# Attention kernel on one core: the read of turned probabilities moved behind three more key pages in each turn, apart from the read of the next queries

## Chip, core and metric

The kernel runs on one core of one Trainium2 chip. The metric is the device time of one execution in microseconds (us). Three runs before the change gave 1230.02, 1235.01 and 1238.47 us; the median, 1235.01 us, is the number to move.

## What is computed

Eight sequences of 128 rows and 512 columns pass through two layers. The first applies one of eight adapter matrices per sequence and a small mixture of low-rank experts. The second, where nearly all the time goes, is attention over a paged cache, followed by a gated low-rank layer. Cut to the attention, the reference is:

```python
q, k, v = x @ Wq.T, x @ Wk.T, x @ Wv.T           # 32 query heads, 8 key and value heads, 128 wide
q, k = rope(rmsnorm(q, q_norm_w)), rope(rmsnorm(k, k_norm_w))
kc = k_cache[block_table].reshape(B, 512, 8, 128) # 16 pages of 32 keys for each sequence
vc = v_cache[block_table].reshape(B, 512, 8, 128)
scores = einsum("bqhd,bkhd->bhqk", q, repeat(concat(kc, k), 4)) * SCALE
probs = softmax(where(valid, scores, -1e30))
o = einsum("bhqk,bkhd->bqhd", probs, repeat(concat(vc, v), 4))
out = o.reshape(B, S, 4096) @ Wo.T
```

All arithmetic is 32-bit.

## The kernel before, in words

The attention is cut into 64 units, one for each sequence and key head. Two units in a row share a sequence and form a step `st`; a step's keys are one tile `kt` of 16 pages (buffer count 2) and one tile `vt` of values. A key head serves four query heads, h = 0 to 3. The function `iteration(u)` (line 1225) is one turn of a software pipeline over the units: in turn u the scores and the softmax of unit u are made, the projections for a unit about three ahead, the product with the values for unit u - 2 at the end of the turn, and the output product of unit u - 3. Nothing is reordered by a scheduler: each engine runs its instructions in the order in which the Python code issues them. The lines that matter are these.

- **Scores.** `scores` on TensorE: lines 837 (against the cached keys `kt`) and 840 (against the new keys), into two PSUM buffers. VectorE takes them out with the mask and the row minimum (850), ScalarE exponentiates (861), VectorE inverts the sum (866), GpSimd scales (867), and VectorE turns the probabilities in 32 by 32 blocks into `pb` (872).
- **The way through DRAM.** The block transpose turns inside blocks only; the order of the blocks is mended by a round trip through a DRAM tile `px`. `exchange_out(u)` (877) writes `pb` there at the end of turn u as four transfers of 400 KB (886), two issued by SyncE (SP) and two by ScalarE (ACT). In turn u + 1, `exchange_in(u)` (892) reads it back, both reads from SP: the turned queries and key of unit u + 2 as `qkb` (896, 320 KB) and the turned probabilities of unit u as `pT` (899, 1280 KB, two buffers, by the parity of u). `qkb` is put into place by ScalarE at the end of the turn (`heads_qk`, 906) and is needed by the first scores of the next turn. `pT` is needed by the product with the values (919) at the end of the next turn, some 14 us after it has landed.
- **One buffer `pb`.** There is one `pb`, so in turn u the first thing that VectorE writes into it, the turned queries of unit u + 2 (`blocks_qk`, 823, called at h = 2), waits until all four writes of turn u - 1 have landed. Behind it on VectorE stand the turned probabilities (872), the adds that take the projections out of PSUM (264, which free the bank that TensorE's next projection, 261, writes) and the scores of h = 3 (850).
- **Pages.** `gather` (185) issues the key pages of the step after this one from SP, 32 KB each (196), every one behind a read of its page number into a register. An even turn issues ten pages, an odd turn six: the first three ahead of `exchange_in`, the rest behind it. The last six pages of a step are issued in the odd turn, and TensorE reads that `kt` in the first score product of the even turn that follows.
- **Other traffic from SP.** In one odd turn out of two a partial output is read back (146), in the other it is written (1142). GpSimd issues the value gathers (206) and the weights.
- **Completion semaphores.** In the built program, the transfers of SP and ACT take eight completion semaphores in rotation, in the order in which the code issues them. A transfer whose semaphore was last used by another one waits, ahead of its issue and in its engine's queue, until that other one has landed. Which transfer stands eight places ahead of which therefore depends on the order of the code.

The main loop ends with turn 66; turns 60 and later have no pages or fewer, and the second layer's last part is mixed into them.

Of the kernel before, what the change touches and what calls it, by code (L numbers as in the profile page):

```python
# [9 lines left out]
F32 = mybir.dt.float32  # L10
# [6 lines left out]
P = 128  # L17
# [16 lines left out]
QD = P // 32  # L34
HN = DM // 2
PW = REP * (LC + 1) * 32
# [22 lines left out]
def adaln_ffn_kernel(  # L59
# [25 lines left out]
    nc = tc.nc  # L85
# [33 lines left out]
        out=nw, in_=norm_w.rearrange("o (t d) -> o t d", t=2).to_broadcast([P, 2, D])  # L119
# [65 lines left out]
    def gather(step, first=0, end=NPP):  # L185
        hf, b = divmod(step, B)
        if first == 0:
            kv_t[step] = (
                kvp.tile([P, NPP, GH, PSIZE], F32, tag="kt", name=f"kt_{step}"),
                kvp.tile([P, LC, GH * D], F32, tag="vt", name=f"vt_{step}", bufs=3),  # L190
            )
        kt, vt = kv_t[step]
        for j in range(first, end):
            at = b * NPP + j
            page = nc.sync.value_load(pg[0:1, at : at + 1])
            nc.sync.dma_start(
                out=kt[:, j, :, :].rearrange("p g t -> p (g t)"),
                in_=kc[hf, ds(page, 1)].rearrange("o p f -> p (o f)"),
            )
# [198 lines left out]
    with ExitStack() as l0:  # L398
# [70 lines left out]
        for i in range(QD):  # L469
            nc.gpsimd.dma_start(  # L470
                out=vpg[i * 32 : (i + 1) * 32], in_=vpages[i : i + 1].to_broadcast([32, B * LC])
# [319 lines left out]
    with ExitStack() as l1:  # L791
        wk1 = l1.enter_context(tc.tile_pool(name="l1_1", bufs=1))
# [7 lines left out]
        p_t, pb_t, pT_t, den_t, o_t, oT_t, y_t = {}, {}, {}, {}, {}, {}, {}  # L800
        mask_t, px_t, qkb_t, qk_out = {}, {}, {}, {}
# [89 lines left out]

        def exchange_in(u):
            m = px_t.pop(u).rearrange("k b i f -> (k b) i f")
            if u + 2 in range(3, NU):
                qkb = wk1.tile([P, QD, NH * 32], F32, tag="qkb", name=f"qkb_{u + 2}")
                nc.sync.dma_start(out=qkb, in_=m[:, :, PW:])
                qkb_t[u + 2] = qkb
            pT = wk1.tile([P, QD, PW], F32, tag=f"pT{u % 2}", name=f"pT_{u}")
            nc.sync.dma_start(out=pT, in_=m[:, :, :PW])
            pT_t[u] = pT  # L900

        def heads_qk(u):

# [278 lines left out]
        def room(b):  # L1182
            at = [0]

            def sb(n, shape):
                if n in ("yT", "zg", "zT"):
                    v = room_t[n, b if n != "yT" else b % 2]
                    return v if len(shape) == 2 else v.rearrange("p (c s) -> p c s", c=shape[1])
                at[0] += -(-shape[1] // 8) * 8
                return room_t["small", b % 2][:, at[0] - -(-shape[1] // 8) * 8 :][:, : shape[1]]  # L1190

            def psum(n, shape):
                t = bank("kv" if n == "z" else "q", f"f{n}_{b}")
                if len(shape) == 2:
                    return t[:, : shape[1]]
                t = t[:, : shape[1] * shape[2]]
                return t.rearrange("p (c s) -> p c s", c=shape[1])

            return sb, psum
# [25 lines left out]
        def iteration(u):  # L1225

            on = lambda v: 0 <= v < NU
            fb = LAST.get(u)
            r, group = u % 16, (u // 16 + 1) * GH
            f = room(fb) if fb is not None else None  # L1230

            if u % 4 == 3:
                k, j, four = (u + 5) // 4, 0, True
            elif u % 4 == 0:
                k, j, four = (u + 4) // 4, 0, False
            elif u % 4 == 1:
                k, j, four = (u + 3) // 4, 1, True
            else:
                k, j, four = (u + 2) // 4, 1, False
# [3 lines left out]
            st = u // GH  # L1243
            pages = on(u) and 1 < st + 1 < NQ * B
            first, end = ((0, 10), (10, NPP))[u % GH]
            if pages:
                gather(st + 1, first, first + 3)
            if on(u - 1):
                exchange_in(u - 1)
            if pages:  # L1250
                gather(st + 1, first + 3, end)
            if pages:
                gather_v(st + 1, u % GH * LC // GH, (u % GH + 1) * LC // GH)
            if on(u + 3) and u % GH == 1:
# [100 lines left out]
        for u in range(NU + 3):  # L1355
            iteration(u)
# [160 lines left out]
```

## Time and profile before

| what | us |
|---|---|
| median of three runs | 1235.01 |
| profiled execution, its own time | 1233.53 |
| span of that execution | 1231.8 |
| key pages, 32 KB each, issued one by one | 512 |
| a pair of turns in the loop | 31 to 36 |
| SP waits at the writes to `px` for an earlier write to `px` | 60.5 in 24 waits |
| bytes moved | 302.71 MB, 246 GB/s over the span |

How to read it: times in a timeline are counted from the span's start, and the execution's own time is 1.7 us more than its span. The granted TensorE clock was 0.999 of full speed, so no part of the time is a slower clock. Busy shares of TensorE contain a modelled end, so where its stalls matter the distance between starts of its instructions is used. The waits of SP's queue (marked SPq) cost nothing by themselves; they matter by when a transfer starts.

### The profile page before, as it was taken

Reading aid. Unit: us, or ns where it says so; the run is one execution under the profiler, and the core shown is the slowest. Engines: PE = TensorE matmul, PEld = TensorE weight load, DVE = VectorE, ACT = ScalarE, POOL = GpSimd, SP = SyncE. Lnnn points to the kernel's source line nnn. Section 1 sums busy time; section 2 is a strip of 40 time slices with the busy share of each in tenths; the row PEclk is TensorE's granted clock in tenths of the full one; section 3 lists DMA queues with packets and bytes.
Section 4 is the critical chain, followed back from the end, with each engine's and each line's share of the span. In section 5 each row is a group of like instructions: output and inputs, shape, how many; then the busy total and the mean of one; then the engine's idle time right before and its main releaser. Section 6 shows DMA issues by size and latency. Waiting matters only on the chain.

```text
span 1231.8 us, 16787 instructions
## 1 busy us (share of the span) xinstructions
PE 1205.3 (98%) x4159; PEld 708.9 (58%) x4159; DVE 908.4 (74%) x2099; ACT 504.0 (41%) x1457; POOL 718.5 (58%) x800
## 2 busy tenths in 40 slices
PE   8999989999999999999999999999999999999998
PEld 7765545565555555555555565555555555655544
DVE  2545778878888787788887787888786888876622
ACT  1344444444444443444444344444443444443211
POOL 2443678778755576577646675687556775742100
PEclk9999999999999999999999999999999999999999
DMA  8822688888888988898889888988888888878742
GB/s 305 298 88 95 215 243 247 257 258 277 253 251 257 288 253 234 282 281 282 248 260 284 267 241 277 291 285 253 255 262 262 263 263 257 263 259 235 218 130 95
DMA packets 206837, 302.71 MB, mean 246 GB/s; under 512 B 84820, under 2 KB 120405, under 8 KB 205845
## 3 DMA queue, kind: packets, MB, share of 16 engines
q1 hardware_dynamic: 174964, 208.72, 53.8%
q10 hardware_dynamic: 18720, 52.32, 16.2%
q0 software_dynamic: 13056, 40.60, 9.7%
q8 instruction: 33, 0.54, 0.2%
q14 instruction: 64, 0.52, 0.1%
HBM read 185.64 MB, written 115.93 MB: 245 GB/s over the span
## 4 chain that ended last, share of the span: by engine, by line
PE 50%; DMA 19%; POOL 8%; DVE 8%; issue 6%; SPq 4%; ACT 4%; ACTq 0%; DVEq 0%; POOLq 0%
DMA px<-pb 14%; PE o L919 10%; PE p L261 9%; PE s L837 9%; PE y L1044 6%; DVE pb L872 3%; DMA kt<-in_kc 3%; POOL p L867 3%; PE bp L548 2%; PE op L1404 2%; PE s L840 2%; PE cp L526 2%; ACT sq L310 2%; PE y L1057 2%; PE fz L733 2%
## 5 line engine op out<-in xcount | busy, mean ns | idle before, releaser
L861 ACT ACTIVATE p<-p,low 128x640 f32<-128x640 f32 x256 | 211.7, 827 | 467.2 <-DVE den L866 299.2
L867 POOL TENSOR_SCALAR p<-p,den 128x640 f32<-128x640 f32 x256 | 209.6, 819 | 275.0 <-DVE den L866 273.6
L261 PE MATMUL p<-wqkv,xo 128*128 128x384 f32 x784 | 283.1, 488 | 4.7 <-DVE c L264 4.6
L850 DVE CUSTOM_DVE_ANT_0 p<-s,mask,rs 128x640 f32<-128x640 f32 x256 | 222.0, 877 | 81.7 <-PE s L840 80.6
L837 PE MATMUL s<-kt,qkT 128*128 128x512 f32 x504 | 259.4, 596 | 11.3 <-DVE low L850 4.9
L919 PE MATMUL o<-pT,vt 128*128 128x512 f32 x512 | 231.6, 595 | 0.0
L872 DVE STREAM_TRANSPOSE pb<-p 128x640 f32<-128x640 f32 x256 | 211.0, 824 | 18.8 <-POOL p L867 18.8
L1044 PE MATMUL y<-wo,oT 128*128 128x256 f32 x784 | 206.6, 380 | 0.5 <-DVE yp L1113 0.5
L261 PEld LDWEIGHTS p<-wqkv,xo 128*128 128x128 f32 x784 | 147.6, 190 | 76.2 <-DVE c L264 11.3
L840 PEld LDWEIGHTS s<-qkT 128*128 128x128 f32 x504 | 95.8, 190 | 120.5 <-issue 120.5
L919 PEld LDWEIGHTS o<-pT,vt 128*128 128x128 f32 x512 | 98.0, 191 | 111.3 <-issue 96.3
L206 POOL DMA_INDIRECT vt<-in_vc,vrow x128 | 141.9, 1108 | 34.4 <-issue 32.0
L837 PEld LDWEIGHTS s<-kt,qkT 128*128 128x128 f32 x504 | 93.1, 190 | 85.8 <-issue 38.3
L1044 PEld LDWEIGHTS y<-wo,oT 128*128 128x128 f32 x784 | 131.8, 191 | 9.4 <-PE s L840 0.6
L310 ACT ACTIVATE sq<-c 128x128 f32<-128x128 f32 x320 | 98.8, 309 | 8.1
L840 PE MATMUL s<-qkT 128*128 128x128 f32 x504 | 96.8, 274 | 0.0
L823 DVE STREAM_TRANSPOSE pb<-ca 128x640 f32<-128x640 f32 x60 | 50.4, 840 | 55.7 <-DMA px<-pb 53.4
L316 POOL TENSOR_TENSOR rs<-ss,mhalf 128x5 f32<-128x5 f32 x64 | 83.7, 1308 | 5.3
L942 ACT COPY oT<-o 128x512 f32<-128x512 f32 x64 | 37.5, 585 | 91.0 <-PE o L919 65.4
L314 POOL TENSOR_SCALAR ss<-ss,eps 128x5 f32<-128x5 f32 x64 | 20.7, 323 | 77.6 <-ACT sq L310 77.4
L919 PE MATMUL o<-pT,vn 128*128 128x512 f32 x128 | 65.4, 592 | 0.0
L264 DVE TENSOR_TENSOR c<-c,p 128x384 f32<-128x384 f32 x84 | 44.9, 534 | 21.3 <-PE p L261 21.0
(193 smaller groups left out, 1409.1 us busy)
## 6 DMA issues: line engine op xcount, KB each, us to landing
pT<-px SPq DMA_DIRECT2D x64, 1280.0 KB
px<-pb ACTq DMA_DIRECT2D x120, 400.0 KB
px<-pb SPq DMA_DIRECT2D x120, 400.0 KB
qkb<-px SPq DMA_DIRECT2D x61, 320.0 KB
kt<-in_kc SPq DMA_DIRECT2D x512, 32.0 KB
wqkv<-in_wqkv POOLq DMA_DIRECT2D x32, 384.0 KB
wo<-in_wo POOLq DMA_DIRECT2D x17, 512.0 KB
yd<-yp SPq DMA_DIRECT2D x12, 512.0 KB
```

The costliest lines, as they stand in the source:

```text
L206: nc.gpsimd.indirect_dma_start(out=kv_t[step][1][:, c, :], out_offset=None, in_=vc, in_offset=bass.IndirectOffsetOnAxis(ap=vrow[:, hf, at ...
L261: nc.tensor.matmul(out=ps, lhsT=xo[:, pr, x, c, :], rhs=w[:, c, :], start=(c == 0), stop=(c == 1))
L310: nc.scalar.activation(sq, cs[:, at : at + D], AF.Square, accum_out=ss[:, h : h + 1])
L316: nc.gpsimd.tensor_tensor(rs, ss, mhalf, ALU.pow)
L837: nc.tensor.matmul(out=s[:, :L], lhsT=qkT[:, h, :], rhs=kt[:, :, g % GH, :], start=True, stop=True)
L840: nc.tensor.matmul(out=s[:, L:NK], lhsT=qkT[:, h, :], rhs=qkT[:, REP, :], start=True, stop=True)
L850: nc.vector.tensor_tensor_reduce(out=p, in0=s_t.pop((u, h))[:, :NK], in1=mask_t[st], scale=rs_t[u][:, h : h + 1], scalar=BIG, op0=ALU.add, ...
L861: nc.scalar.activation(p, p, AF.Exp, bias=low, scale=-1.0, accum_out=den)
L867: nc.gpsimd.tensor_scalar(p_t[u, h], p_t[u, h], den, 1.0, ALU.mult, ALU.mult)
L872: nc.vector.transpose(pb_t[u][:, :, h * w : (h + 1) * w].rearrange("p i (j a) -> p j i a", a=32), p_t.pop((u, h)).rearrange("p (j i a) -> ...
L919: nc.tensor.matmul(out=o, lhsT=vt[:, c, j * D : (j + 1) * D] if c < LC else vn_t.pop(u), rhs=pT[:, c], start=(c == 0), stop=(c == LC),)
L1044: nc.tensor.matmul(out=y_t["y"][:, half * HN : (half + 1) * HN], lhsT=part(key)[:, i * S : (i + 1) * S], rhs=wo_t[:, slot(w, key[0] // (B ...
```

## The change

The two reads of `exchange_in` become two functions. `exchange_qk(u - 1)` reads `qkb` where both reads stood before, behind the turn's first three pages. Three more pages follow, then `exchange_in(u - 1)` with the read of `pT` alone, then the pages that are left: four in an even turn, none in an odd one. No transfer is added, removed or resized.

```diff
         def exchange_in(u):
             m = px_t.pop(u).rearrange("k b i f -> (k b) i f")
+            pT = wk1.tile([P, QD, PW], F32, tag=f"pT{u % 2}", name=f"pT_{u}")
+            nc.sync.dma_start(out=pT, in_=m[:, :, :PW])
+            pT_t[u] = pT
+
+        def exchange_qk(u):
+            m = px_t[u].rearrange("k b i f -> (k b) i f")
             if u + 2 in range(3, NU):
                 qkb = wk1.tile([P, QD, NH * 32], F32, tag="qkb", name=f"qkb_{u + 2}")
                 nc.sync.dma_start(out=qkb, in_=m[:, :, PW:])
                 qkb_t[u + 2] = qkb
-            pT = wk1.tile([P, QD, PW], F32, tag=f"pT{u % 2}", name=f"pT_{u}")
-            nc.sync.dma_start(out=pT, in_=m[:, :, :PW])
-            pT_t[u] = pT
...
             if on(u - 1):
+                exchange_qk(u - 1)
+            if pages:
+                gather(st + 1, first + 3, first + 6)
+            if on(u - 1):
                 exchange_in(u - 1)
             if pages:
-                gather(st + 1, first + 3, end)
+                gather(st + 1, first + 6, end)
```

In the rotation of the semaphores the three pages now stand between `qkb` and `pT`. In the built program before, in 29 even turns (2 to 58) one of SP's two writes to `px`, mostly the first, comes eight places behind ACT's first write of the same turn and waits for it to land, and in most of these turns ACT's second write waits for the turn's `pT`. In the program after, the writes to `px` of the even turns to 58 stand behind pages, but for SP's second write, which stands behind the turn's `pT`.

## Prediction

> **What bounds the kernel now.** I read the busy row of the page first, then the loop's window, then what TensorE waited for.
>
> ```profile
> PE 1205.3 (98%) x4159; PEld 708.9 (58%) x4159; DVE 908.4 (74%) x2099; ACT 504.0 (41%) x1457; POOL 718.5 (58%) x800
> ```
>
> ```profile
> core 0: us, PE busy (x) PEld busy (x) DVE busy (x) ACT busy (x) POOL busy (x), PEclk, DMA share, GB/s
> ...
> 166.00:1120.00 954.00, 943.44 (x3129) 553.06 (x3127) 769.99 (x1688) 420.65 (x1248) 631.72 (x677) 1.00 0.86 263
> ```
>
> TensorE is the bound: in the loop it is busy 943.4 of 954 us at full clock. So a gain can only come out of its gaps, while a loss has no ceiling. Busy time hides part of a gap (the modelled end runs into it), so I also summed the distances between starts of matmuls above the median distance of their kind: 16.8 us from 200 us to the end, 8.2 us from 150 to 200 us. A little over 20 us is the ceiling; I ask which of it the change can reach.
>
> TensorE's own waits, and a place where one happens (the turn boundary into turn 50):
>
> ```profile
> PE s L837 <- DMA kt<-in_kc: 4.4, 4, 1.9
> ```
>
> ```profile
> 924.04 1.02 PE L919 MATMUL o<-pT,vn 128*128 128x512 f32 x2
> 926.94 1.10 PE L837 MATMUL s<-kt,qkT 128*128 128x512 f32 x2 [1.88 <-DMA kt<-in_kc]
> ```
>
> The first score product of an even turn waits for key pages. SP's queue in the odd turn before it:
>
> ```profile
> 916.98 0.54 SPq L896 DMA_DIRECT2D qkb<-px  x1
> 917.57 0.62 SPq L899 DMA_DIRECT2D pT<-px  x1
> 918.72 2.94 SPq L196 DMA_DIRECT2D kt<-in_kc  x3
> 923.68 0.81 SPq L886 DMA_DIRECT2D px<-pb  x2
> ```
>
> The last three pages are issued right behind the 1280 KB of pT, on the same queue. In the packet records pT's last packet ends at 925.6 and the last page's at 925.9, 5.5 us after its issue; the product starts 1.0 us later.
>
> **Part 1: pages ahead of pT.** For every even turn I took the start of its first score product less the start of the last value product before it. With nothing to wait for this is 0.43 us (turns 32, 38, 40 and others). In 18 of the 29 even turns from 4 to 60 it is more, up to 2.47 (turn 50); the excess adds up to 8.7 us. In each of these 18 the last page lands 0.8 to 1.25 us ahead of the product, and the queries lie ready (qkT's copy ends 3 us or more earlier), so it is the pages. After the change the last page of an odd turn goes out at qkb + 0.54 + 0.52 (register read) + 2 x 0.85 = 2.8 us, for turn 49 at 919.7. Pages with no large transfer ahead of them land in about 1.3 to 2.5 us: 922.2 at the latest, where TensorE asks at 924.9. In turn 21, the tightest I found, 461.1 against 463.4. The margin is over 2 us, so all of it goes: **-8.7 us** (ends -8.7 and, if another wait stands right behind, 0). In even turns three pages of ten go ahead as well, but these are asked for a turn later and gain nothing.
>
> **Part 2: the writes of even turns.** SP's queue in turn 30:
>
> ```profile
> 605.50 0.54 SPq L896 DMA_DIRECT2D qkb<-px  x1
> 606.09 0.62 SPq L899 DMA_DIRECT2D pT<-px  x1
> 607.24 6.00 SPq L196 DMA_DIRECT2D kt<-in_kc  x7
> 615.83 0.92 SPq L886 DMA_DIRECT2D px<-pb  x2
> ```
>
> ACT's two writes go out at 612.38 and 612.73, so the data were ready; SP is through with its pages at 613.24 and yet issues at 615.83. By the wait list of the built program its first write shares a completion semaphore with ACT's first write and waits for that to land. The bandwidth while only ACT's writes move (turn 30), and while both queues' do (turn 29):
>
> ```profile
> core 0: us, PE busy (x) PEld busy (x) DVE busy (x) ACT busy (x) POOL busy (x), PEclk, DMA share, GB/s
> 597.30:602.00 4.70, 4.31 (x18) 3.05 (x19) 4.67 (x11) 1.07 (x2) 4.07 (x4) 1.00 0.98 308
> ...
> 613.30:617.40 4.10, 4.10 (x18) 2.72 (x17) 3.57 (x9) 0.93 (x2) 3.58 (x4) 1.00 0.99 199
> ```
>
> The DMA share is full in both, but the rate is 199 GB/s for one queue and 308 for two. The Trainium skill (DMA: Bandwidth & Descriptors, "Issuing engines are not separate DMA queues") speaks against a gain here: transfers of all engines share the same 16 DMA engines, so a second issuer saves issue time only. By that rule the 1.6 MB land as late as before, part 2 is 0 and the sum below 1228.3; by the rows two queues move them half again as fast. I take the rows. After the change this wait is gone: SP's first write goes out at 613.4, its second when pT has landed (issued at 608.65, and 5.2 us later, since its 6.1 us now hold 0.9 us behind qkb: 613.9). 1.1 us of ACT alone moves 0.22 MB, the other 1.38 MB at 308 take 4.5 us: landing near 618.9 instead of 621.65.
>
> Who waits for that: VectorE at line 823 of the next, odd turn, in every odd turn, 1.7 us on average.
>
> ```profile
> DVE pb L823 <- DMA px<-pb: 53.4, 33, 3.2
> ```
>
> The worst, in turn 35, and what it does to TensorE through the add of line 264:
>
> ```profile
> 689.54 0.84 DVE L823 STREAM_TRANSPOSE pb<-ca 128x640 f32<-128x640 f32 x1 [3.20 <-DMA px<-pb]
> ```
>
> ```profile
> 691.60 1.56 PE L261 MATMUL p<-wqkv,xo 128*128 128x384 f32 x4 [0.88 <-DVE c L264]
> ```
>
> VectorE itself is not the bound; only TensorE's stalls behind it count. By distance of starts they are 2.56 (turn 3), 0.70 (13), 0.60 (19), 1.05 (35) and 0.56 (51), 5.5 us in all. Not all goes: **-4 us** (ends -5.5 and 0).
>
> **Part 3: what comes later.** pT is now issued three pages later: 3 x 0.85 us, about 2.6. It has the time: turn 30's pT lands at 612.2 and is read at 626.65. SP issues as many instructions as before, so what stands behind pT (pages, line 146, line 1142, the writes) gets its turn no later. But pT's data move later, some 1.7 us, since they no longer queue behind qkb (packets began 2.3 us after issue behind qkb, and qkb's own 1.35 us after issue). In odd turns they now run up to the writes: in turn 29 pT's packets ended at 596.0, the writes' began at 597.3. So pT would end near 597.7, 0.4 us into them. In the odd turns with line 146, 512 KB more stand between. Against that, part 2 starts the odd turn's reads up to 2.7 us earlier, which covers all of it. If that cover is gone, the writes of odd turns land 0.4 to 1.5 us later and line 823 of even turns is late. There TensorE has little room: after the add of line 264 its next projection starts 0.57 us later in turn 30, 0.16 in turn 48; I use 0.3. Cost then: up to 29 x (1.0 - 0.3) = 20 us. A stall removed on TensorE also takes room from VectorE in the same turn. I put **+2 us** (ends -0.6, for a stall of 0.64 us in turn 28, and +20).
>
> **Sum:** -8.7 - 4 + 2 = -10.7. On the profiled execution 1233.5 - 10.7 = 1222.8; on the median of the runs, 1.5 us above it, 1235.0 - 10.7 = **1224.3 us**.
>
> **Rivals.**
> - *Pages alone.* Part 1 works, part 2 buys nothing (the rule above, or the landing is not what TensorE feels): 1235.0 - 8.7 + 1 = 1227. For it: VectorE's 53 us of waits cost TensorE only about 5. Against: the 199 and 308.
> - *Another wait takes the place.* At the turn boundary the scores also need VectorE to have emptied their PSUM buffer, and VectorE is busy 770 of 954 us. Then the gaps reappear a few us further on: 1233 to 1236. Against: the boundary distance is exactly 0.43 in 11 turns, with nothing behind the pages.
> - *Slower: the odd turns' writes stand behind pT.* One mechanism, at line 823 of even turns, as priced in part 3. It cancels part 1 once these writes land 0.6 us later on average (8.7 / 29 + 0.3); at 1.0 us the time is 1235.0 + 20 - 8.7 = 1246. For it: the DMA engines are 86% busy, and after the change they have only 96 KB of SP's to move in the 2.6 us in which three pages are issued. Against: the qkb of odd turns should start earlier, not later.
>
> **Numbers.** My forecast 0.53 (its own range 1218 to 1230), pages alone 0.22, another wait 0.10, slower 0.15. About 1% is what a measurement of this kernel can tell from no change: 12.35 us, so below 1222.7 or above 1247.4. Somewhat over half of my forecast's case lies below that, and a little of pages alone: 0.33. Of the slower case two thirds go over: 0.10. The rest, 0.57, lies within. The range 1216 to 1240 leaves out most of the slower case and the tail below.
>
> **What would show it.** Part 1: the distance at the boundary into even turns is 0.43 us throughout, and no wait of line 837 for kt is left. Part 2: in even turns SP issues its writes within 1.5 us of ACT's, and line 823's wait for px falls from 53 us to under 20. Part 3: the packets of pT in odd turns end no later than before. I am wrong if line 823 waits more in even turns, or if TensorE's gaps in the loop stay near 10 us.

## The result, and the profile after

The change made the kernel slower: 1253.56 us, median of five runs (1249.47 to 1260.93), against 1234.37 us for five runs of the kernel before beside them. The ratio is 1.0153, with a 95% interval of 1.0121 to 1.0185. The forecast was 1224.3, the range 1216 to 1240. The profiled execution is the slowest of the five (1260.93 us, span 1259.2), so sums over its trace come out some 7 us larger than the medians do.

The busy row of the page after, and the loop's window in one row (its head names the columns); before, about the same turns took 954 us, 166 to 1120:

```profile
PE 1211.5 (96%) x4159; PEld 714.3 (57%) x4159; DVE 908.0 (72%) x2099; ACT 501.6 (40%) x1457; POOL 721.0 (57%) x800
```

```profile
core 0: us, PE busy (x) PEld busy (x) DVE busy (x) ACT busy (x) POOL busy (x), PEclk, DMA share, GB/s
166.00:1145.00 979.00, 948.00 (x3120) 556.99 (x3119) 767.25 (x1683) 416.86 (x1244) 633.29 (x676) 0.99 0.80 256
```

No engine has more instructions. TensorE's 4.6 us more of busy time are about what the clock gives: the granted clock of this execution was 0.994, that of the profile before 0.999, and half a per cent of 943 us is 4.7. The clock is not the cause of the loss, though: the run with the median time, 1253.56 us, had 0.999 too. The loop is 25 us longer, most of it with TensorE idle, and the DMA engines are *less* busy (0.80 for 0.86). So something is late, not more.

TensorE's waits after (engine, line and tile; what it waited for; us in total, times, longest):

```profile
PE p L261 <- DVE c L264: 13.4, 13, 2.5
PE y L1047 <- DVE yp L1116: 11.3, 7, 2.4
PE s L837 <- DVE low L850: 7.2, 4, 2.7
PE s L837 <- ACT qkT L909: 3.3, 5, 1.6
```

The wait for key pages is no longer in the list. The boundary into turn 50, in the timeline after, is closed (0.86 us between the starts of 922 and 837, against 2.90 before):

```profile
947.19 1.02 PE L922 MATMUL o<-pT,vn 128*128 128x512 f32 x2
948.05 1.02 PE L837 MATMUL s<-kt,qkT 128*128 128x512 f32 x2
```

In its place stand two waits for VectorE's adds: line 264, which was 4.6 us, and line 1116 (the add of an output product), which was 0.5 us as line 1113. What VectorE waits for after:

```profile
DVE pb L823 <- DMA px<-pb: 52.5, 31, 4.5
DVE pb L823 <- DMA kt<-in_kc: 42.0, 14, 5.4
```

The second line is the same wait under another name: `blocks_qk` needs no key page, but pages and writes share completion semaphores, and the profile names a transfer that came late. In the packet records line 823 starts 0.5 to 1.0 us behind the last packet of the writes in these turns too (5 to 58). Together 94.5 us, where before had 55.2 us (53.4 and, under the name of key pages, 1.8). The waits are in both kinds of turn now. Turn 28, an even one, from VectorE to TensorE (which by then is at the start of turn 29) in the timeline:

```profile
581.58 0.84 DVE L823 STREAM_TRANSPOSE pb<-ca 128x640 f32<-128x640 f32 x1 [3.77 <-DMA px<-pb]
...
588.22 1.18 DVE L1116 TENSOR_TENSOR yp<-yp,y 128x1024 f32<-128x1024 f32 x1
```

```profile
589.55 2.04 PE L1047 MATMUL y<-wo,oT 128*128 128x256 f32 x4 [1.67 <-DVE yp L1116]
```

Line 823 waits 3.8 us for the writes of the odd turn 27; VectorE does not catch up by 588, its add of line 1116 frees a PSUM bank late, and TensorE stands 1.7 us. The eight largest stalls of this kind, four or eight turns apart, are 1.5 to 2.6 us each by distance of starts.

SP's queue after, odd turn 29 and the even turn 30, in the timeline:

```profile
598.05 0.53 SPq L902 DMA_DIRECT2D qkb<-px  x1
599.10 2.06 SPq L196 DMA_DIRECT2D kt<-in_kc  x3
601.50 0.53 SPq L895 DMA_DIRECT2D pT<-px  x1
605.70 0.81 SPq L886 DMA_DIRECT2D px<-pb  x2
...
615.46 0.53 SPq L902 DMA_DIRECT2D qkb<-px  x1
616.51 2.03 SPq L196 DMA_DIRECT2D kt<-in_kc  x3
618.63 0.53 SPq L895 DMA_DIRECT2D pT<-px  x1
619.68 2.86 SPq L196 DMA_DIRECT2D kt<-in_kc  x4
622.64 2.77 SPq L886 DMA_DIRECT2D px<-pb  x2
```

By the packet records, pT of turn 29 ends at 607.30, which is 1.6 us behind the issue of both queues' writes; their last packet ends at 614.81, 9.1 us after the issue.

**The table for all runs.** Each number is a mean over turns 5 to 58, worked out from the issue times and packet records of one profiled execution. *SP behind ACT*: SP's first write to `px` less ACT's first. *Landing*: last packet of the four writes less their first issue (in odd turns this is ACT's packet, on average: 7.78 us before and 9.09 after, where SP's two writes end at 6.29 and 8.25). *pT past writes*: last packet of the turn's pT less the first issue of its writes (negative: pT was out of the way). *823*: the start of line 823 less the end of VectorE's instruction before it, that is the time for which VectorE was idle there (where nothing waits it can come out a hair under 0). Times are medians; the ratio is to before on the same chip, and as the medians of before lie between 1234.4 and 1239.3 from chip to chip, different rows are best compared by their ratios. All in us.

| kernel | time | ratio | even: SP behind ACT | even: landing | odd: 823 | odd: pT past writes | odd: landing | even: 823 |
|---|---|---|---|---|---|---|---|---|
| before | 1234.4 | 1 | 3.52 | 9.60 | 1.62 | -0.06 | 7.97 | 0.20 |
| after | 1253.6 | 1.015 | 0.49 | 9.60 | 1.99 | 2.27 | 9.17 | 1.48 |
| even turns only | 1227.7 | 0.992 | 0.13 | 8.61 | 0.88 | -0.46 | 8.03 | 0.16 |
| odd turns only | 1261.0 | 1.017 | 3.58 | 9.63 | 2.09 | 2.33 | 9.26 | 1.76 |
| after, half of pT | 1226.5 | 0.992 | 0.29 | 8.95 | 1.31 | 0.04 | 8.15 | 0.57 |
| odd only, half of pT | 1230.0 | 0.993 | 3.03 | 9.54 | 1.75 | 0.44 | 8.06 | 0.45 |
| odd: six pages first | 1280.4 | 1.033 | 1.75 | 9.37 | 2.00 | 2.26 | 10.28 | 2.01 |
| the same, with even turns | 1269.3 | 1.024 | 0.42 | 9.31 | 2.03 | 1.73 | 9.61 | 1.63 |
| one page between | 1257.7 | 1.016 | 3.61 | 9.55 | 1.55 | 1.18 | 8.65 | 0.15 |
| 13 and 3 pages | 1273.2 | 1.026 | 5.98 | 11.27 | 3.52 | -0.03 | 8.05 | 0.76 |
| even only, 11 and 5 pages | 1250.8 | 1.012 | 0.98 | 10.20 | 2.18 | -0.25 | 7.98 | 0.25 |
| rotation moved by one | 1247.9 | 1.009 | 4.12 | 9.93 | 2.02 | 0.00 | 8.02 | 0.22 |
| four pages in one issue | 1215.3 | 0.983 | -0.09 | 7.70 | 0.21 | -1.27 | 7.79 | 0.00 |
| three pages by GpSimd | 1235.7 | 1.001 | -0.06 | 7.63 | 0.25 | -1.08 | 7.86 | -0.01 |

### The profile page after: what moved, and what is told of

Same layout as the page of the kernel before. It is cut to its first block, busy times and chain, and to the rows that moved or that the text cites. A ratio compares the mean times of both kernels' runs of the same rounds, so it can differ in the third digit from the quotient of the medians.

```text
span 1259.2 us, 16781 instructions
## 1 busy us (share of the span) xinstructions
PE 1211.5 (96%) x4159; PEld 714.3 (57%) x4159; DVE 908.0 (72%) x2099; ACT 501.6 (40%) x1457; POOL 721.0 (57%) x800
## 4 chain that ended last, share of the span: by engine, by line
PE 47%; DMA 24%; POOL 8%; DVE 7%; issue 7%; SPq 4%; ACT 3%; ACTq 0%; DVEq 0%; POOLq 0%
DMA px<-pb 15%; PE o L922 10%; PE p L261 8%; PE s L837 7%; PE y L1047 6%; DMA pT<-px 5%; DVE pb L872 3%; DMA kt<-in_kc 3%; POOL p L867 3%; PE bp L548 2%; PE op L1411 2%; PE y L1060 2%; PE cp L526 2%; PE s L840 2%; PE fz L733 2%
## 5 line engine op out<-in xcount | busy, mean ns | idle before, releaser
L1047 PE MATMUL y<-wo,oT 128*128 128x256 f32 x784 | 210.3, 386 | 13.5 <-DVE yp L1116 11.3
L1116 DVE TENSOR_TENSOR yp<-yp,y 128x512 f32<-128x512 f32 (+3 forms) x94 | 59.9, 638 | 0.0
```

Source lines behind the costliest of these rows:

```text
L1047: nc.tensor.matmul(out=y_t["y"][:, half * HN : (half + 1) * HN], lhsT=part(key)[:, i * S : (i + 1) * S], rhs=wo_t[:, slot(w, key[0] // (B ...
```

## Experiments

**Theory A** (called D from the second series on): pT of odd turns is late; its data stand in front of the next writes on SP's queue, these land later, and line 823 of the following even turn waits. **Rival B** (E later): the new order of issues and semaphores itself costs it. **Rival C**: some other wait took the place.

### The change in half of the turns

```diff
             if on(u - 1):
                 exchange_qk(u - 1)
-            if pages:
+            if pages and u % GH == 1:
                 gather(st + 1, first + 3, first + 6)
             if on(u - 1):
                 exchange_in(u - 1)
             if pages:
-                gather(st + 1, first + 6, end)
+                gather(st + 1, first + 6 if u % GH == 1 else first + 3, end)
```

This is the edit for the odd turns alone; for the even ones `u % GH == 0` stands in both places. The odd turns alone:

> The three pages go between the two reads in odd turns only; even turns are as before. Theory A (late pT: its data, 2.5 us later, lie in front of the same turn's writes to px, so VectorE's line 823 of the next turn is late and TensorE starves behind it): the waits for pages vanish (-8.7 us) and only the even turns' line 823 gets later, more than half of the loss: 1240 to 1247 us, boundary distance 0.43 us, TensorE's new gaps in even turns alone. Rival B (the changed rotation of the semaphores in even turns is what costs): even turns keep their old neighbours, no loss, 1225 to 1229 us.

Measured: 1261.04 us, ratio 1.0171 (1.0125 to 1.0217). That is as slow as the whole change (1.0153, with an interval that overlaps). The odd turns hold the whole loss; B, which sought it in the even turns, falls. The size is above what A gave.

The even turns alone:

> The three pages go between the two reads in even turns only; odd turns are as before. Theory A: the waits for pages at the boundary stay (no gain), the writes of even turns land no earlier, line 823 of odd turns gets later: 1240 to 1248 us, new gaps in odd turns at line 261. Rival B (rotation in even turns): the whole loss without the gain, above 1255 us. My forecast's part 2, had it held: 1229 to 1232 us.

Measured: 1227.71 us, ratio 0.9916 (0.9876 to 0.9957): faster, which neither A nor B had expected, but what part 2 of the forecast would have been by itself. TensorE's waits in this kernel:

```profile
PE s L837 <- DVE low L850: 4.5, 3, 2.4
PE s L837 <- DMA kt<-in_kc: 4.1, 3, 2.0
PE p L261 <- DVE c L264: 3.2, 2, 2.9
```

The key pages still cost what they did (8.3 us by distance of starts over all even turns, 8.7 before), and next to nothing waits at the output product. The gain goes with the writes of even turns, which land 1.0 us earlier. This is the best kernel here that computes the whole reference, and it beats both.

### One page in place of three, and a split that needs no page behind pT

```diff
-                gather(st + 1, first + 3, first + 6)
+                gather(st + 1, first + 3, first + 4)
```

> One page between the two reads instead of three, in both turns; pT goes out some 0.85 us later instead of 2.55. Theory A with the loss in proportion to pT's lateness beyond a small slack: loss of at most a third of 28 us, and two of the odd turn's last pages still behind pT, so most waits for pages stay: 1236 to 1243 us. Rival B (any change of the rotation or splitting of the reads costs): as slow as three pages, 1250 us or more.

Measured: 1257.65 us, ratio 1.0157 (1.0111 to 1.0203). pT past the writes and the landing stand between before and after, as A says, and line 823 of even turns does not wait. The time is lost elsewhere: two pages of the odd turn are still behind pT, which is now later itself, and by distance of starts the key pages cost some 28 us at the turn boundary, 19 more than before, which is about the loss of this run (18 us against before on its chip). My figure had left that out.

The next one keeps before's order and gives even turns 13 pages, odd turns three, so that no page of the odd turn is behind pT:

```diff
-            first, end = ((0, 10), (10, NPP))[u % GH]
+            first, end = ((0, 13), (13, NPP))[u % GH]
```

> The kernel before with 13 pages in even turns and 3 in odd ones instead of 10 and 6: no page of a step stands behind pT in the odd turn, and both reads stay together at their old place. Theory A: the waits for pages vanish and pT is not late, so 1225 to 1230 us, unless the even turn's ten pages behind pT hold up SP's writes to px beyond the old 3.5 us behind ACT's. Rival C (with the pages gone from the boundary another wait takes their place whatever pT does): 1233 to 1237 us.

Measured: 1273.17 us, ratio 1.0261 (1.0225 to 1.0298): the clause behind "unless" came about. Ten pages behind pT put SP's first write 6.0 us behind ACT's, the even writes land at 11.3 us, and line 823 of odd turns waits 3.5. TensorE's longest sum of waits:

```profile
PE p L261 <- DVE c L264: 37.8, 26, 3.2
```

Each page on SP goes out 0.85 us after the one before, so three more of them behind pT put the writes some 2.5 us later.

### pT's bytes

The odd turns as in the change, but with half of pT's bytes; first with even turns as before, then in the whole change. This is the edit of the second; the first has `if u < 4:` in place of `if u < 4 or u % 2:`, and leaves the even turns' three pages where they were:

```diff
+        pT_keep = {}
...
-            pT = wk1.tile([P, QD, PW], F32, tag=f"pT{u % 2}", name=f"pT_{u}")
-            nc.sync.dma_start(out=pT, in_=m[:, :, :PW])
+            if u < 4 or u % 2:
+                pT_keep[u % 2] = wk1.tile([P, QD, PW], F32, tag=f"pT{u % 2}", name=f"pT_{u}")
+            pT = pT_keep[u % 2]
+            w = PW // 2 if 4 <= u < 60 and u % 2 == 0 else PW
+            nc.sync.dma_start(out=pT[:, :, :w], in_=m[:, :, :w])
```

> Edit: odd turns as in the change and even turns as before, which alone took 1261 us; of that, in the odd turns the read of pT fetches only half of each row's probabilities from unit 4 to unit 59 (the other half keeps an earlier unit's values, so this part of the computation is left out). The order of the issues and the rotation of the semaphores stay. Theory D: the loss is the time that pT's bytes take in front of the px writes, so with half of them the odd px writes land about 8.0 to 8.4 us after the first issue instead of 9.3, line 823 of even turns waits under 0.6 instead of 1.8 us, and the time is 1230 to 1240 us. Rival E (the issue order and the rotation themselves cost it): 1255 or more. Between 1240 and 1255 both have a part.

Measured: 1229.97 us, ratio 0.9931 (0.9904 to 0.9957). Same issues, same order, same semaphores as the odd turns alone, and 31 us less (2.4% by the ratios). pT ends 0.44 us past the writes' issue in place of 2.33, the odd writes land at 8.06 us, line 823 of even turns waits 0.45. E falls. Half of pT in 28 turns also takes 18 MB, 6%, out of all that the kernel moves; but the even writes hardly feel it (9.54 us for 9.63), so the help is in the odd turns and not everywhere.

> Edit: the whole change, with only half of each row's probabilities read by pT in the odd turns from unit 4 to unit 59 (the other half keeps an earlier unit's values, so this part of the computation is left out). Theory D (the whole change loses by pT's bytes of the odd turns, which stand in front of the next px writes; its other parts gain): the odd px writes land at 8.0 to 8.5 us instead of 9.2, line 823 of even turns waits under 0.6 instead of 1.5 us, the even px writes land at 8.6 to 9.0 instead of 9.6, and the time is 1218 to 1230 us, ratio 0.985 to 0.995, against 1254 of the whole change. Rival E (the three pages and the order cost it): 1245 or more.

Measured: 1226.53 us, ratio 0.9916 (0.9888 to 0.9944), 27 us less than the whole change (2.4% by the ratios). The even writes now land at 8.95 us and line 823 of even turns waits 0.57 us. With half of the bytes the change comes out where I had put it, 10.7 us below before (on this chip 1237.2); that the sum agrees to a tenth is luck, as the parts do not agree so well. The list of TensorE's waits is back to small ones:

```profile
PE s L837 <- DVE low L850: 4.7, 3, 2.4
PE p L261 <- DVE c L264: 4.6, 5, 2.5
PE y L1052 <- DVE yp L1121: 2.8, 2, 1.7
```

So it is shown that the loss is the time that pT's bytes take ahead of the writes. Whether they stand in the way on SP's queue or in the DMA engines, these runs do not separate, as halving the bytes eases both; the packet records go further. ACT's writes go through a queue of their own, and in the odd turns alone they too send their first packet 2.51 us after their issue, for 1.53 before (1.67 with half of pT); SP's take 2.42, for 1.10 (1.27). And the writes that land last are ACT's, at 9.18 us, where SP's end at 8.08. The order on SP's queue alone can't be the cause, then: pT also holds back what another queue carries. How the DMA engines do that is not shown.

### All six pages of the odd turn ahead of both reads

If lateness of pT *against qkb* were the trouble, putting the pages ahead of both would cure it.

```diff
+            ahead_of = first + 3 if u % GH == 0 else end
             if pages:
-                gather(st + 1, first, first + 3)
+                gather(st + 1, first, ahead_of)
             if on(u - 1):
                 exchange_in(u - 1)
             if pages:
-                gather(st + 1, first + 3, end)
+                gather(st + 1, ahead_of, end)
```

> Edit: even turns as before the change; in odd turns all six pages go ahead of both reads. Theory D: only the waits for key pages of line 837 fall away, 18 of 29 of them, 8.7 us in all by TensorE's excess, and the px writes of even turns still wait behind ACT's first: 1226 to 1231 us, ratio 0.993 to 0.998. Rival E: both reads are now some 2.5 us later in odd turns against the writes, so that odd px writes land 1.2 us later as in the change: 1250 or more. Rival F (the key pages never set the end): 1234, ratio 0.999 to 1.001.

> Edit: even turns as in the change (three pages between the two reads); in odd turns all six pages go ahead of both reads, so that no page stands behind pT there and pT follows qkb at once. Theory D (the loss is pT's data in odd turns standing in front of the next turn's px writes on SP's queue; the gain of the even turns is SP's first px write no longer waiting behind ACT's): the even turns keep what they had alone (even px writes land some 8.6 us after the first issue, line 823 of odd turns waits 0.9 instead of 1.6 us), and the waits for key pages of line 837 (8.7 us in all before) fall to nothing: 1228 less some 5 to 8 = 1219 to 1224 us, ratio 0.987 to 0.992. Three more pages in front of qkb may make it up to 0.5 us later in 30 odd turns, which D counts at nothing to 4. Rival E (any six pages ahead of pT's read in odd turns push pT and with it the writes, wherever qkb stands): pT lands as late as in the change, 1250 or more.

The second does the same in odd turns and has the change's order in even ones. Measured: 1280.4 us, ratio 1.0334 (1.0300 to 1.0368), and 1269.25 us, ratio 1.024 (1.0201 to 1.0278), the slowest of their series. My figures for D were wrong in both; E's number came true. SP's queue in one odd turn of the first:

```profile
458.48 0.84 SPq L886 DMA_DIRECT2D px<-pb  x2
460.71 6.10 SPq L196 DMA_DIRECT2D kt<-in_kc  x6
466.91 0.54 SPq L896 DMA_DIRECT2D qkb<-px  x1
467.51 0.62 SPq L899 DMA_DIRECT2D pT<-px  x1
471.46 0.81 SPq L886 DMA_DIRECT2D px<-pb  x2
```

The six pages take 6.1 us to issue and end just as the reads go out. On average qkb is issued 2.63 us after the writes have landed; before it was 0.62. I had written "up to 0.5 us". With qkb late, ScalarE's copy waits too (50.7 us in 29 waits, for qkT; 4.5 us in 5 before). In the first of the two pT ends 2.3 us past the writes' issue, as in the change, so these runs agree with the mechanism and not with the cure that I tried: pT is late whether the pages stand between the reads or ahead of both. The first lands its odd writes 1.1 us later than the change does at the same end of pT; what adds that is open.

### The even turns' gain

Three tries at getting it without moving pT. (In the built program ACT's writes stand among SP's pages of the same turn, ahead of the last of them; how many SP issues follow ACT's first write before SP's own decides who takes up its semaphore.) First, one added small read on SP, to move the rotation of semaphores by one:

```diff
-            if pages:
+            if pages and u % GH == 0:
+                gather(st + 1, first + 3, first + 8)
+                nc.sync.dma_start(out=ids, in_=lora_ids)
+                gather(st + 1, first + 8, end)
+            elif pages:
                 gather(st + 1, first + 3, end)
```

> Edit: the kernel before, with one added read of a few bytes on SP among the seven pages behind pT in even turns (it loads the same small table of ids again, which nothing needs any more). It moves the rotation of the completion semaphores by one, so that SP's first px write of most even turns waits behind a key page instead of behind ACT's first write; neither read is moved. Theory D: this is all that makes the even turns faster, so the even px writes land about 1 us sooner (8.6 instead of 9.6), the wait of line 823 in odd turns falls from 1.6 to about 0.9 us, and the time is 1225 to 1230 us, ratio 0.991 to 0.996. Rival G (the gain came from pT's later read in even turns, which leaves the queue free for qkb and the first writes): 1234 to 1238, with the landing at 9.6. Third: the added read's issue, one more among SP's, costs up to 0.1 us in 30 turns, 3 us, if SP's issues set the pace there.

Measured: 1247.89 us, ratio 1.0091 (1.0056 to 1.0127): slower. The wait that it was to remove is still there. In most even turns SP's write no longer shares a semaphore with ACT's first, but a key page ahead of it on SP does now, and SP waits all the same:

```profile
581.24 4.38 SPq L196 DMA_DIRECT2D kt<-in_kc  x5
585.67 0.32 SPq L1252 DMA_DIRECT2D ids<-in_lora_ids  x1
588.05 2.99 SPq L196 DMA_DIRECT2D kt<-in_kc  x2
591.14 1.23 SPq L886 DMA_DIRECT2D px<-pb  x2
```

ACT's first write of that turn goes out at 586.31; SP's follow 4.8 us later. The wait moved by one place, and the page ahead of it now waits for the turn's pT. The key pages cost more as well: 13.5 us by distance of starts, for 8.6 before (turns 6 to 58). To let SP's write pass, the issues between it and ACT's first can be made fewer. In this run the last four of the seven pages behind pT are one issue:

```diff
+    def gather_run(step, first, end):
+        hf, b = divmod(step, B)
+        kt, vt = kv_t[step]
+        nc.sync.dma_start(
+            out=kt[:, first:end].rearrange("p j g t -> p j (g t)"),
+            in_=kc[hf, first:end].rearrange("o p f -> p o f"),
+        )
...
+            if pages and u % GH == 0:
+                gather(st + 1, first + 3, first + 6)
+                gather_run(st + 1, first + 6, end)
+            elif pages:
                 gather(st + 1, first + 3, end)
```

> Edit: the kernel before, with the last four of the seven pages behind pT in even turns fetched by one issue of the same bytes (it takes four neighbouring pages instead of those that the table names, so the look-up of these pages is left out). Neither read is moved. Three issues fewer stand between ACT's first px write and SP's, so SP's writes no longer take up the semaphores of ACT's writes of their own turn. Theory D (the waits of SP's queue behind ACT's first write make the px writes of even turns late, and the gain of the even turns comes from their end): SP's first write issues within 0.5 us of ACT's instead of 3.5 behind it, the even px writes land at 8.4 to 8.9 us, line 823 of odd turns waits 0.7 to 1.0 us, and the time is 1224 to 1230 us, ratio 0.989 to 0.995. Rival G (the even turns gained by pT's later read itself): 1233 to 1238, with the landing at 9.4 or more. If the merged read is slower than four, the waits of line 837 grow and the time with them.

Measured: 1215.27 us, ratio 0.9831 (0.9802 to 0.9860), below what D gave. SP's writes go out with ACT's, the even writes land at 7.7 us, line 823 waits next to nothing in either turn, and the pages behind pT in odd turns are in time too, since everything ahead of them is earlier. G falls: the gain needs no later pT. (This run leaves the look-up of those pages out, so it is no replacement for the kernel.) The busy row and TensorE's longest wait here:

```profile
PE 1198.9 (99%) x4159; PEld 713.7 (59%) x4159; DVE 909.9 (75%) x2099; ACT 505.0 (42%) x1457; POOL 714.9 (59%) x800
```

```profile
PE s L845 <- DVE low L858: 4.1, 3, 2.4
```

The gain is the sum of things that this run does not part: SP's wait for ACT's write is gone, SP spends 0.42 us on one issue where four pages take 3, and the four pages are neighbours.

The same with every page looked up, and three of them issued by GpSimd:

```diff
-            if pages:
-                gather(st + 1, first + 3, end)
+            if pages:
+                gather(st + 1, first + 3, end - 3 if u % GH == 0 else end)
+                if u % GH == 0:
+                    gather(st + 1, end - 3, end, nc.gpsimd)
```

> Edit: the kernel before, with the last three of the seven key pages behind pT in even turns issued by GpSimd instead of SP, every page still looked up in the table. Neither read is moved. Theory D (the seven pages on SP's queue hold its px writes of even turns back; with four neighbouring pages in one issue this was worth 1.7%): SP's first write issues within 0.5 us of ACT's, even px writes land at 7.7 to 8.5 us instead of 9.6, the waits of line 837 for key pages are under 3 us in all, and the time is 1216 to 1226 us, ratio 0.983 to 0.991. Against it stands GpSimd's own work: three look-ups and issues in each of 30 even turns, by the 1.1 us of one of its value reads some 3 us a turn, and line 867 (the normalizing) queues behind them; if GpSimd's normalizing then sets when line 872 and the px writes come, 1235 to 1260.

Measured: 1235.70 us, ratio 1.0009 (0.9992 to 1.0026): no change. The writes are as early as in the run before (7.63 us, line 823 waits 0.25), so that part of D came true, and its time did not. GpSimd's group for the pages (busy, mean ns, idle time before), and three waits that grew (before, line 872's was 18.8 us in 64, the one for line 850 was 4.9 us, and the one for line 166 was not in the list):

```profile
L196 POOL DMA_DIRECT2D kt<-in_kc x90 | 51.8, 575 | 75.1 <-issue 72.3
```

```profile
DVE pb L872 <- POOL p L867: 34.9, 79, 3.2
```

```profile
PE s L837 <- DVE low L850: 9.2, 4, 3.4
PE p L261 <- POOL wqkv L166: 4.8, 3, 1.9
```

A page costs GpSimd 1.4 us with its look-up, and the normalizing and the weights' sums stand behind it. That this is what ate the gain is what these waits point to; no run shows it by itself.

Last, the even turns' half with one page moved over from the odd turn, to shorten the boundary waits that were left:

```diff
-            first, end = ((0, 10), (10, NPP))[u % GH]
+            first, end = ((0, 11), (11, NPP))[u % GH]
...
-                gather(st + 1, first + 3, first + 6)
+                gather(st + 1, first + 3, first + 7)
```

> Edit: even_only with one key page moved from the odd turn to the even turn (11 and 5 in place of 10 and 6): three pages, the next queries, four pages, pT, four pages in even turns; three pages, both reads, two pages in odd turns. Theory D: the last pages of a stage land 0.85 us sooner against its end, which leaves next to nothing of the waits for key pages (8.3 us by TensorE's excess in even_only); pT of even turns comes 0.85 us later, which the 1 us of lead of the even turns' writes covers: 1220 to 1226 us, ratio 0.984 to 0.991. Rival H (each page in front of pT makes the even px writes later by its 0.85 us): even landing 9.2 or more, odd waits of line 823 of 1.4 or more, 1230 to 1240.

Measured: 1250.78 us, ratio 1.0119 (1.0076 to 1.0163). Rival H came true, beyond its numbers: landing 10.2 us, odd waits of 2.2. The key pages did cost less (4.4 us by distance of starts, for 8.2 in the even turns' half, both over turns 6 to 58). pT, one page later, ends 3.85 us past the even writes' issue (1.92 in the even turns' half), and SP's second write, which shares its semaphore, goes out at 4.3 us in place of 2.4. One page decided between 0.8% of gain and 1.2% of loss: the even turns' half stands at the edge of its slack.

## Why the prediction was wrong

The forecast was -8.7 - 4 + 2 us. By the runs the whole change is -8.7 for part 1, nothing for part 2 and, as what is left of the measured 19.2, about +28 for part 3.

**Part 1 was right.** The distance at the boundary is 0.43 us in every even turn after, and no wait for pages is left. The 8.7 us were there, and were gained.

**Part 2 was right in kind by itself, and did not survive part 3.** In the even turns' half SP's first write goes out 0.13 us behind ACT's in place of 3.52, the writes land 1.0 us sooner (I had put 2.7), and line 823 of odd turns waits 0.74 us less; this is worth 0.8% there, nearly all of it without part 1. By the medians that is 11.6 us (5 to 15 by the interval) where I had put 4 and at most 5.5; the spans of the two profiled executions differ by 5.9 us (1231.8 and 1225.9). Which is nearer is open. The rule weighed there (the Trainium skill, DMA: Bandwidth & Descriptors, "Issuing engines are not separate DMA queues") gave nothing for this step; that the same 1.6 MB land 1.0 us sooner is on the side of the rows. In the whole change the writes land at 9.60 us as before. SP's first does go out early (0.49), but its first packet only 3.3 us later (1.9 before), behind pT; ACT's first packet, on the other queue, comes 2.6 us after its issue (1.0 before). SP's second write waits for pT to land:

```profile
SPq L886 <- DMA pT<-px: 66.1, 30, 3.8
```

The coupling: the late writes of odd turns make VectorE wait at line 823 of even turns, so that from the issue of qkb to the first write of the same even turn pass 6.85 us and no longer the 7.52 of the even turns' half. The reads start when the writes have landed, VectorE too; with no slack between them, pT has 0.7 us less to get out of the way. I had counted on 5.2 us from pT's issue to its landing here; it was 6.4.

**Part 3 is the step that failed**, in two sentences of it. "pT's data move later, some 1.7 us, since they no longer queue behind qkb": the time from pT's issue to its landing is 6.2 us after, with qkb out of the way, as it was 6.2 in odd turns before. (I had read 2.3 us from its issue to its first packet behind qkb; by the packet records it was 1.9, and 1.3 after, so that its packets began 0.6 us sooner and yet ended no sooner.) The whole later issue (2.56 us) less a little is lateness: pT ends 2.27 us past the odd writes' issue, where it ended 0.06 us before it. That is 2.3 us and not 1.7, and the odd writes land 1.2 us later, where I had put 0.4 and a cover for it. "Part 2 starts the odd turn's reads up to 2.7 us earlier, which covers all of it": there was nothing to cover with, as the even writes land no sooner in the whole change; and it would not have covered all, since starting the reads earlier starts VectorE's line 823, and with it the writes, earlier too. In the even turns' half, where the even writes did land 1.0 us sooner, pT of odd turns gained 0.4 us on its writes (-0.06 to -0.46). I put +2 us on a cost whose own upper end was +20; it came to about +28.

**The price of lateness was near.** The slower rival charged 29 x (lateness - 0.3) us for odd writes that land late, less part 1. The odd turns alone were late by 9.26 - 7.97 = 1.29 us: 29 x 0.99 - 8.7 = +20 us, measured +22 (1261.0 against 1239.3). The whole change was late by 1.20: +17.4, measured +19.2. With six pages first in odd turns it gives +50 for 2.31 us, measured +43, and with one page between, 0.68 us late, line 823 of even turns doesn't wait at all; so the formula, with its 0.3 us chosen between two readings, comes near in these three and is no rule. The rival's mechanism and place were the true ones, and I gave it 0.15 because of a cover that isn't one. The argument that I had against it, "the qkb of odd turns should start earlier", concerns the start of the turn, and the collision is between two things that both hang on that start.

## What to carry to other kernels

When a read is moved later on a queue, compare its end with the issue of what follows *in the same turn*, on the other queues too; an earlier start of the turn moves both and covers little (0.4 of 1.0 us here). A lateness hidden from its own reader (pT had 14 us of slack there) is still paid by the transfers issued next to it. Where a queue's issues are dense (0.85 us a page here), fewer issues can be worth more than another order of them: four pages in one issue, without their look-up, were worth 1.7%, and of the eight new orders of SP's issues tried here (the change among them) one gained, 0.8%.

## What was not expected of the hardware

- The wait for a shared completion semaphore was not removed by shifting the rotation by one: another instruction ahead on the same queue took that semaphore and waited in its place (4.12 us of SP behind ACT, for 3.52). It went when three issues fewer stood between the two (-0.09 us).
- One issue of 128 KB took SP 0.42 us, four issues of 32 KB about 3 us.
- In odd turns the 1280 KB of pT took 6.17 us from issue to landing with 320 KB issued 0.62 us ahead of them on the same queue, and 6.23 us when it was issued just after these had landed, with three pages in between.
- A large read on SP's queue held back the writes on ACT's queue as well: with pT 2.3 us past their issue, ACT's first packet came 2.43 us after its issue in odd turns of the whole change, for 1.53 before.
